# Halving the last units of a graph-convolution kernel, and weighing three of its last pairs on VectorE

## The chip, the cores and the metric

The kernel runs on one core of one Trainium2 chip. The metric is device time in microseconds. The profile's times (us) are counted from the start of the profiled execution's span; the lines (L415 and so on) are those of the kernel before.

## The reference

```python
h = max(layernorm(x), 0)                       # x: 4096 x 64
support = h @ weight                           # 64 x 64
mask = (adj != 0)                              # adj: 4096 x 4096, 64 MB in float32
rank = cumsum(mask, axis=1); deg = rank[:, -1:]
k = min(deg, 100); pos = rank - (deg - k)
w = mask * where(pos > 0, 0.5 ** (k - pos), 0)
out = x + w @ support + bias
```

A neighbour of a row therefore has a weight that halves with every later neighbour in that row: the last one weighs 1, the one before it 1/2, and those beyond the hundredth from the end nothing. To know the weight of a column one must know how many neighbours follow it, so the columns are worked from the right.

## The kernel before

**Units.** The 4096 rows form 8 groups of 512. Each group is worked in two units of 2048 columns, the right half first (L81), which makes 16 units, 0 to 15. A unit is loaded as four tiles of 128 rows by 2048 columns (1 MB each), so there are 64 tiles, 0 to 63. Unit 14 is the right half of the last group and unit 15 the left half.

**One unit's stages, with the function, line and engine of each.**

1. *load* (L118, SyncE's DMA queue) brings a tile into one of the 8 buffers of `apool`. A buffer is free again once its tile has been converted.
2. *convert* (L339, VectorE) turns float32 into bytes. For the tile numbers in `signed` it is L337 on ScalarE instead.
3. *transpose* (L350, TensorE) and *settle* (L361, VectorE) turn the bytes by 90 degrees, so that columns lie on partitions, and bring them back from PSUM to SBUF. PSUM tiles of tag "t" for this and for the next stages come from two banks, used in turn.
4. *totals* (L367, TensorE) counts neighbours in blocks of columns. *split* (L377, ScalarE) and *divide* (L380, VectorE) fetch one byte plane each of the same PSUM bank; in the program one of them always waits for the other. For a left half *carry* (L386, GpSimd) puts in the count of the right half, taken from `behind` of the unit before. *suffix* (L394, TensorE) and *clamp* (L398, VectorE) make from this `behind`, the number of later neighbours.
5. *place* (L405 and L410, TensorE) writes for four pairs at a time, 0 to 3 and then 4 to 7, a PSUM tile `v` whose bytes are the exponents. There are five banks for `v`, so the next place waits until three of the four pairs before it have been weighed.
6. *weigh* (L415, ScalarE) reads two byte planes of one `v`, 128 x 1024 elements, and writes exp(-ln 2 (38 + byte)), the weight, as `wk`. The factor 2 to the -38 is made good in the supports (L284). There are 8 pairs in a unit, 128 in all.
7. *aggregate* (L427, TensorE) multiplies `wk` with the supports `hr`, two matmuls to a pair, and adds up one group in the PSUM tile `acc`.
8. After a left half *drain* (L440), *turn_back* (L447) and *finish* (L454, L455) add the bias, turn the result back and add x. Only the last group does this in two halves of its rows: one drain on VectorE (L438), one on ScalarE (L440), and two stores (L457).

**What sets the order.** Each engine executes its instructions in the order in which they were written into the program. A list scheduler at the end of the function (L490 to L607) makes that order at build time: each task has an engine, a due time (its position in the stream of tiles, with the corrections in `shift` and `own`), costs in ns, and the tasks and buffers that it needs. It takes one task after the other and calls the functions in that order. None of this runs on the chip, so an instruction whose inputs are late holds up all that stand behind it on its engine.

Of the kernel before, what the change touches and what calls it, by code (L numbers as in the profile page):

```python
# [8 lines left out]
F32 = mybir.dt.float32  # L9
# [22 lines left out]
def kernel(  # L32
# [48 lines left out]
    UNITS = [(g, c * P * E, n) for g in range(G) for c, n in ((4, 4), (0, 4))]  # L81
# [4 lines left out]
    NP = 2 * CB  # L86
    NA = 8
# [21 lines left out]
    xt = apool.tile([P, N // H], F32, tag="a_sb", name="xt")  # L109
# [20 lines left out]
    junk = setup.tile([P, W], BF16, name="junk")  # L130
# [112 lines left out]
    def warm(n):  # L243

        for i in range(n):
            nc.tensor.matmul(none, junk[:, :P], junk, start=True, stop=True)  # L246
# [28 lines left out]
    def spread(n):  # L275
        if n == 0:
            pxs["var"] = ps_v.tile([P, W], F32, tag="v", name="pd")
        for b in range(4 * n, 4 * n + 4):
            nc.tensor.matmul(pxs["var"][:, H * b:H * (b + 1)], sq[:, b, :], ones, start=True, stop=True)  # L279
# [46 lines left out]
    masks, words, wts, accs, tots, pts, sums8, behind, vs, signed = {}, {}, {}, {}, {}, {}, {}, {}, {}, (2, 3, 5, 6, 12)  # L326
# [86 lines left out]
    def weigh(u, k):  # L413
        wts[u, k] = wpool.tile([P, 2, W], F32R, name="wk")
        nc.scalar.activation(wts[u, k], vs.pop((u, k)).bitcast(U8).rearrange("p (i f) -> p f i", f=4)[:, :2, :], AF.Exp, scale=-LN2, bias=floor)  # L415
# [5 lines left out]
    def aggregate(u, k):  # L421
# [3 lines left out]
        wk = wts.pop((u, k))  # L425
        for s in range(2):
            nc.tensor.matmul(accs[g], hr[:, block(u, k) + 4 * s, :, :].rearrange("p s d -> p (s d)"), wk[:, s, :],  # L427
                             start=(k == s == 0 and c0 + cb * E * P == N), stop=(c0 == 0 and (k, s) == (2 * cb - 1, 1)))
# [30 lines left out]
    def store(r):  # L459
# [8 lines left out]
    shift = {"aggregate": 56.5, "carry": -33, "center": -22.5, "clamp": -3, "constants": 17.5, "convert": 38.5, "drain": -32.5,  # L468
             "finish": -27, "first": -5.5, "order_of": -3, "place": 1, "power": -38.5, "relu": 13, "root": 21, "scale": 32.5,
             "second": 66, "settle": -19.5, "split": -26, "spread": -11.5, "square": 8.5, "suffix": 15.5, "support": 28.5,  # L470
             "totals": -2.5, "transpose": 1, "turn": 15, "turn_back": 55, "turned": 13.5, "weigh": 17.5}
    own = {
           "aggregate": {(0, 0): 6, (0, 1): 10, (0, 2): -1, (0, 4): -11, (0, 5): 21, (0, 6): -8, (0, 7): -1, (1, 0): -1, (1, 1): -1, (1, 3): 7, (1, 4): -8, (1, 5): -1},
           "carry": {(1,): -20}, "center": {(0,): 26, (1,): 62, (2,): 2, (3,): 1}, "clamp": {(0,): -2, (1,): 8, (2,): -1},
           "constants": {(0,): 5, (1,): -2},
           "convert": {(10,): -1, (11,): -16, (12,): -10, (13,): 12, (14,): -15, (15,): 12, (2,): 20, (3,): -8, (4,): -31, (7,): -6, (8,): -7, (9,): 2},
           "count": {(2,): 1, (4,): -10}, "counted": {(2,): -18, (4,): -19},
           "first": {(0, 0): -2, (0, 1): 19, (1, 0): -2, (1, 1): -9}, "order_of": {(2,): 4},
           "place": {(1, 0): 2, (1, 1): -8, (2, 0): 16}, "relu": {(0,): 24, (1,): 1, (3,): 2}, "root": {(): -17},
           "scale": {(1,): 12, (2,): 1, (3,): -5}, "second": {(0, 0): -2, (0, 1): -12, (1, 0): -5},  # L480
           "settle": {(0,): 5, (1,): -8, (10,): 5, (11,): 15, (12,): 4, (13,): 1, (14,): 21, (2,): -5, (3,): -8, (4,): 8, (5,): -4, (6,): -1, (7,): 24, (8,): 5, (9,): -2},
           "split": {(1,): 6, (2,): 2}, "spread": {(0,): -5, (1,): 1, (2,): 4, (3,): 1}, "square": {(0,): 2, (1,): 10, (2,): 4},
           "suffix": {(0,): -8, (1,): 20}, "support": {(0,): 5, (2,): -3, (3,): 8}, "totals": {(0,): 14, (1,): -8},
           "transpose": {(0, 2, 4): 4, (1, 0, 2): -3, (1, 2, 4): -6, (10, 0, 2): -7, (10, 2, 4): -6, (11, 0, 2): 16, (11, 2, 4): 5, (12, 0, 2): 8, (12, 2, 4): -5, (13, 0, 2): 8, (13, 2, 4): 4, (14, 0, 2): -1, (14, 2, 4): -8, (2, 0, 2): -11, (3, 0, 2): -2, (3, 2, 4): -4, (4, 0, 2): 26, (4, 2, 4): 19, (5, 0, 2): 6, (5, 2, 4): -3, (6, 0, 2): 4, (6, 2, 4): 14, (7, 0, 2): 14, (7, 2, 4): -1, (8, 0, 2): 4, (9, 2, 4): -6},
           "turn": {(0, 0): -2, (0, 12): 5, (0, 4): 5, (0, 8): 16, (1, 0): -10, (1, 12): -9, (1, 4): -8, (1, 8): 6},
           "turned": {(0, 12): 12, (0, 4): -4, (1, 0): 4, (1, 12): 16, (1, 8): 8},
           "weigh": {(0, 0): 11, (0, 1): -2, (0, 2): -4, (0, 3): -1, (0, 4): 8, (0, 6): 3, (0, 7): -1, (1, 0): -6, (1, 2): -18, (1, 3): 8, (1, 4): 4, (1, 6): -8}}
# [11 lines left out]
    for n in range(NT):  # L499
        slot = ("center", 3) if n == NA - 1 else ("convert", n - NA) if n >= NA else None  # L500
        task(load, (n,), SP, n, 0, 0, [slot])
# [143 lines left out]
```

## Time and profile before

| | |
|---|---|
| median of 8 runs | 193.39 us (192.66 to 195.26) |
| the profiled execution's own time | 192.9 us |
| its span, first to last instruction | 191.2 us |
| what lies around the span | 1.7 us |
| busy in the span | TensorE 171.0, ScalarE 167.4, VectorE 153.7, GpSimd 12.9 us |
| bytes moved | 69.47 MB, some 420 GB/s until 165 us |
| last convert (L339) | 168.10 to 169.48 us |
| first stores of the last group are issued | 187.99 us |

Busy time says how long an engine had an instruction in work, not that it set the time. A wait is named by what the engine waited for last. The chain that ended last is followed back from the last instruction to what released it.

### The profile page before, as it was taken

Reading aid. Unit: us, or ns where it says so; the run is one execution under the profiler, and the core shown is the slowest. Engines: PE = TensorE matmul, PEld = TensorE weight load, DVE = VectorE, ACT = ScalarE, POOL = GpSimd, SP = SyncE. Lnnn points to the kernel's source line nnn. Section 1 sums busy time; section 2 is a strip of 40 time slices with the busy share of each in tenths; the row PEclk is TensorE's granted clock in tenths of the full one; section 3 lists DMA queues with packets and bytes.
Section 4 is the critical chain, followed back from the end, with each engine's and each line's share of the span. In section 5 each row is a group of like instructions: output and inputs, shape, how many; then the busy total and the mean of one; then the engine's idle time right before and its main releaser. Section 6 shows DMA issues by size and latency. Waiting matters only on the chain.

```text
span 191.2 us, 3737 instructions
## 1 busy us (share of the span) xinstructions
PE 171.0 (89%) x1473; PEld 101.3 (53%) x1475; DVE 153.7 (80%) x213; ACT 167.4 (88%) x178; POOL 12.9 (7%) x54
## 2 busy tenths in 40 slices
PE   7799995979999998799999997999999889998961
PEld 2475982445546564556455555465555444664630
DVE  4852469999999988998899979999998999954012
ACT  2379988889899999999969999898699999989970
POOL 7000240200010002000010010000100100001000
PEclk9999999999999999999999999999999999999995
DMA  6999999999999999999999999999999999800100
GB/s 219 423 420 423 417 422 422 418 415 423 418 418 420 423 418 420 420 417 423 422 417 422 420 420 422 418 420 420 420 417 417 423 417 420 337 16 4 78 0 27
DMA packets 10337, 69.47 MB, mean 363 GB/s; under 512 B 1360, under 2 KB 1616, under 8 KB 2128
## 3 DMA queue, kind: packets, MB, share of 16 engines
q1 hardware_dynamic: 10016, 69.15, 87.4%
q8 instruction: 11, 0.18, 0.4%
q10 hardware_dynamic: 304, 0.10, 0.2%
q14 instruction: 6, 0.05, 0.1%
HBM read 68.19 MB, written 1.05 MB: 362 GB/s over the span
## 4 chain that ended last, share of the span: by engine, by line
PE 38%; DVE 33%; ACT 16%; issue 8%; POOL 3%; ACTq 0%; POOLq 0%; DVEq 0%
DVE m L339 16%; PE acc L427 14%; ACT wk L415 11%; PE pt L350 8%; DVE mt L361 6%; PE v L410 4%; PE v L405 4%; ACT sums L377 2%; DVE behind L398 2%; PE pc L263 2%; DVE sums L380 2%; PE pd L279 2%; PE tot L367 2%; PE po L447 1%; ACT xt L258 1%
## 5 line engine op out<-in xcount | busy, mean ns | idle before, releaser
L415 ACT ACTIVATE wk<-v,floor 128x1024 fp32r<-128x1024 uint8 x128 | 132.8, 1123 | 6.8 <-PE v L410 6.5
L339 DVE TENSOR_SCALAR m<-a_sb 128x2048 uint8<-128x2048 f32 x59 | 81.6, 1388 | 5.4 <-DMA a_sb<-in_adj_dram 5.4
L427 PE MATMUL acc<-wk,hr 128*128 128x512 f32 x256 | 77.9, 423 | 1.6 <-ACT wk L415 0.5
L427 PEld LDWEIGHTS acc<-wk,hr 128*128 128x128 f32 x256 | 43.8, 189 | 15.2 <-issue 5.0
L350 PE MATMUL pt<-ident,m 128*128 128x128 f32 x256 | 41.5, 282 | 6.5 <-DVE mt L361 2.9
L361 DVE COPY mt<-pt 128x512 uint32<-128x512 uint32 x59 | 40.2, 682 | 5.7 <-PE pt L350 5.7
L350 PEld LDWEIGHTS pt<-ident,m 128*128 128x128 f32 x256 | 27.8, 141 | 26.6 <-issue 9.8
L405 PE MATMUL v<-behind,where 32*128 32x512 f16 x128 | 15.6, 382 | 1.4 <-DVE behind L398 1.4
L386 POOL COPY sums<-behind 1x512 f16<-1x512 f16 x8 | 5.6, 706 | 141.1 <-ACT sums L377 141.1
L380 DVE CAST sums<-tot 128x512 f16<-128x512 uint8 x16 | 10.9, 683 | 4.9 <-ACT sums L377 4.2
L410 PE MATMUL v<-mt,tri 32*32 32x512 f16 x512 | 14.3, 394 | 0.0
L337 ACT ACTIVATE m<-a_sb 128x2048 int8<-128x2048 f32 x5 | 12.6, 2519 | 0.3 <-DMA a_sb<-in_adj_dram 0.3
L398 DVE TENSOR_SCALAR behind<-ps,excess 128x512 f16<-128x512 f32 x16 | 11.9, 742 | 1.2 <-PE ps L394 1.2
L377 ACT ACTIVATE sums<-tot 128x512 f16<-128x512 uint8 x16 | 9.6, 597 | 2.7 <-DVE sums L380 2.3
L394 PE MATMUL ps<-sums,later 128*128 128x512 f16 x32 | 9.7, 381 | 1.5 <-POOL sums L386 1.4
L367 PE MATMUL tot<-mt,band 128*32 128x512 f16 x128 | 10.2, 392 | 0.4
L410 PEld LDWEIGHTS <-tri 32*32 32x32 f16 x512 | 4.4, 88 | 10.3 <-issue 10.3
L246 PE MATMUL none<-junk 128*128 128x512 bf16 x24 | 8.1, 480 | 1.3 <-DVE junk L131 1.2
L405 PEld LDWEIGHTS <-where 32*128 32x128 f16 x128 | 3.6, 91 | 9.5 <-issue 9.3
L258 ACT ACTIVATE xt<-px 64x512 f32<-64x512 f32 x8 | 4.2, 586 | 4.6 <-PE px L254 4.6
L438 DVE TENSOR_SCALAR acc_part<-acc,bias_sb 128x256 f32<-128x256 f32 x1 | 0.5, 484 | 9.5 <-PE acc L427 9.5
L447 PE MATMUL po<-ident,acc_sb 128*128 128x128 f32 x30 | 4.9, 285 | 2.6 <-ACT acc_sb L440 2.5
(82 smaller groups left out, 82.0 us busy)
## 6 DMA issues: line engine op xcount, KB each, us to landing
a_sb<-in_adj_dram SPq DMA_DIRECT2D x64, 1024.0 KB, 16.2
xr<-in_x_dram SPq DMA_DIRECT2D x2, 512.0 KB, 6.2
out_dram<-xr SPq DMA_DIRECT2D x1, 512.0 KB, 18.6
out_dram<-xr SPq DMA_DIRECT2D x1, 384.0 KB, 2.3
out_dram<-xr ACTq DMA_DIRECT2D x1, 64.0 KB, 1.6
out_dram<-xr SPq DMA_DIRECT2D x1, 64.0 KB, 1.6
w<-in_L_gnn_weight_dram ACTq DMA_DIRECT2D x2, 16.0 KB, 5.7
bias_sb<-in_L_gnn_bias_dram SPq DMA_DIRECT2D x1, 0.2 KB, 17.4
```

The costliest lines, as they stand in the source:

```text
L337: nc.scalar.activation(m_v.bitcast(I8), a_v, AF.Sign)
L339: nc.vector.tensor_scalar(m_v, a_v, 0.0, 64.0, op0=ALU.not_equal, op1=ALU.add)
L350: nc.tensor.transpose(pts[n][:, c, :], m32[:, c * P:(c + 1) * P], ident)
L361: nc.vector.tensor_copy(mw, pt)
L367: nc.tensor.matmul(tot[SUB * c:SUB * (c + 1), :], band[:, SUB - 12 - 4 * a:2 * SUB - 12 - 4 * a], masks[u][:, c, :, a], start=(a == 0), st ...
L377: nc.scalar.activation(*bytes_of(u, 0), AF.Copy)
L380: nc.vector.tensor_copy(*bytes_of(u, 1))
L398: nc.vector.tensor_scalar(behind[u], pts.pop((u, "s")), excess[UNITS[u][2]], float(MAX_NEIGH), op0=ALU.subtract, op1=ALU.min)
L405: nc.tensor.matmul(v, where[q, a, :], behind[u][q, :], start=True, stop=False, skip_group_check=True)
L410: nc.tensor.matmul(vs[u, 4 * a + j][SUB * c:SUB * (c + 1), :], tri[q, q], m, start=False, stop=True, skip_group_check=True)
L415: nc.scalar.activation(wts[u, k], vs.pop((u, k)).bitcast(U8).rearrange("p (i f) -> p f i", f=4)[:, :2, :], AF.Exp, scale=-LN2, bias=floor)
L427: nc.tensor.matmul(accs[g], hr[:, block(u, k) + 4 * s, :, :].rearrange("p s d -> p (s d)"), wk[:, s, :], start=(k == s == 0 and c0 + cb * ...
```

## The change

- **Units.** The left half of the last group is cut into two units of 1024 columns: columns 1024 to 2047 (unit 15) and 0 to 1023 (unit 16). Each has four pairs and four tiles of 128 x 1024 (512 KB), so there are now 17 units and 68 tiles, 60 to 67 being half tiles. The second unit width brings a second set of small constants (`thr2`, `later2`, `excess2`) in the setup.
- **Weighing on VectorE.** Three pairs, number 4 of unit 14 and number 0 of units 15 and 16 (`QUICK`), are not weighed on ScalarE. VectorE makes their weights in three steps: *encode* computes max(-2^23 byte, -100 2^23) as int32 from PSUM, *cut* adds 100 2^23, and the result read as float32 is 2 to the (-27 - byte), or 0 from byte 100 on; *take* copies it to `wk`. As this is 2^11 more than ScalarE's weight, *lower* on GpSimd makes copies of their supports times 2^-11, six small instructions. The aggregate of these pairs is called *gather* in the scheduler, and stands at a place of its own.
- **Halves of the rows.** Pairs 2 and 3 of unit 16 (`PARTED`) are weighed and aggregated in two halves of 256 rows: half 0 of both, then half 1 of both.
- **Drains.** The last group's ScalarE drain now comes first, and VectorE's waits for it; before it was the other way round.
- **Elsewhere.** `signed` is (6, 15) and was (2, 3, 5, 6, 12), so ScalarE converts two tiles and not five. `xt`, the turned x, lies in a buffer of the mask pool instead of `apool`, so tile 7's load waits for no buffer. The matmuls on `junk` that keep TensorE busy are half as wide and end at the first *spread*; the variance's PSUM tile is taken from another pool. All numbers of `shift` and `own` are new, so the order of nearly all instructions moves by a little.

```diff
-    UNITS = [(g, c * P * E, n) for g in range(G) for c, n in ((4, 4), (0, 4))]
+    UNITS = [(g, c * P * E, n) for g in range(G) for c, n in (((4, 4), (2, 2), (0, 2)) if g == G - 1 else ((4, 4), (0, 4)))]
...
+    QUICK = (U - 3, 4), (U - 2, 0), (U - 1, 0)
+    PARTED = 2, 3
...
-    xt = apool.tile([P, N // H], F32, tag="a_sb", name="xt")
+    xt = mpool.tile([P, CB, W, 2], F16, name="mt").rearrange("p c i e -> p (c i e)").bitcast(F32)
...
-            pxs["var"] = ps_v.tile([P, W], F32, tag="v", name="pd")
+            pxs["var"] = ps_a.tile([P, W], F32, tag="acc", name="pd")
...
-    def weigh(u, k):
+    def weigh(u, k, part=None):
+        r = slice(0, W) if part is None else slice(part * W // 2, (part + 1) * W // 2)
+        if not part:
+            wts[u, k] = wpool.tile([P, 2, W], F32R, name="wk")
+        v = vs[u, k] if part == 0 else vs.pop((u, k))
+        nc.scalar.activation(wts[u, k][:, :, r], v.bitcast(U8).rearrange("p (i f) -> p f i", f=4)[:, :2, r], AF.Exp, scale=-LN2, bias=floor)
+
+    def encode(u, k):
+
+        both = apool.tile([P, N // H], F32, tag="a_sb", name="code")
+        codes[u, k] = both.rearrange("p (n f i) -> p n f i", n=2, f=2)
+        nc.vector.tensor_scalar(codes[u, k][:, 0].bitcast(I32), vs.pop((u, k)).bitcast(U8).rearrange("p (i f) -> p f i", f=4)[:, :2, :],
+                                -2.0 ** 23, -100 * 2.0 ** 23, op0=ALU.mult, op1=ALU.max)
+
+    def cut(u, k):
+
+        nc.vector.tensor_scalar(codes[u, k][:, 1].bitcast(I32), codes[u, k][:, 0].bitcast(I32), 100 * 2.0 ** 23, None, op0=ALU.add)
+
+    def take(u, k):
         wts[u, k] = wpool.tile([P, 2, W], F32R, name="wk")
-        nc.scalar.activation(wts[u, k], vs.pop((u, k)).bitcast(U8).rearrange("p (i f) -> p f i", f=4)[:, :2, :], AF.Exp, scale=-LN2, bias=floor)
+        nc.vector.tensor_copy(wts[u, k], codes.pop((u, k))[:, 1])
+
+    def lower(u, k):
+
+        if not low:
+            both = apool.tile([P, N // H], F32R, tag="a_sb", name="low").rearrange("p (n s e d) -> p n s e d", s=2, e=2, d=D)
+            low.update((uk, both[:, i]) for i, uk in enumerate(QUICK))
+        for s in range(2):
+            nc.gpsimd.tensor_scalar(low[u, k][:, s, :, :], hr[:, block(u, k) + 4 * s, :, :].bitcast(F32), 2.0 ** -11, None, op0=ALU.mult)
...
+            if (u, k) in QUICK:
+                weighs = "take"
+                task(encode, (u, k), DVE, due - 8, 1150, 1270, [("place", u, k // 4), ("convert", NT - 2)])
+                task(cut, (u, k), DVE, due - 8, 650, 770, [("encode", u, k)])
+                task(take, (u, k), DVE, due - 8, 650, 770, [("cut", u, k)], ("w", ("gather", u, k)))
+                task(lower, (u, k), POOL, due - 8, 1200, 1300, [("second", piece_of // 2, piece_of % 2), ("convert", NT - 3)])
...
+        for part in range(2 if u == U - 1 else 0):
+            for k in PARTED:
+                due = at + k + part
+                task(weigh, (u, k, part), ACT, due + 2.5, 520, 650, [("place", u, k // 4)], None if part else ("w", ("aggregate", u, k, 1)))
+                task(aggregate, (u, k, part), PE, due + 14, 260, 500, [("weigh", u, k, part)])
```

The order that results at the end is, on each engine (a pair is written unit.number, and "a/b" is half a or b of its rows):

- ScalarE: ..., 13.4, split 14, 13.5, 13.6, 13.7, 14.0, split 15, 14.1, drain of group 6, 14.2, 14.3, 14.5, split 16, 14.6, 14.7, 15.1, 15.2, 15.3, 16.1, 16.2 a, 16.3 a, 16.2 b, 16.3 b, drain.
- VectorE: convert 58, settle 57, convert 59, settle 58, convert 60, convert 61, settle 59, convert 62, settle 60, divide 14, settle 61, convert 63, clamp 14, settle 62, convert 64, settle 63, convert 65, settle 64, divide 15, settle 65, convert 66, convert 67, settle 66, finish of group 6, settle 67, encode 14.4, divide 16, clamp 15, cut and take 14.4, encode 15.0, clamp 16, cut and take 15.0, encode, cut and take 16.0, drain.
- TensorE, leaving out the transposes before tile 64: ..., place 14 (first), transpose 64, totals 15, aggregate 13.6, transpose 65, aggregate 13.7, transpose 66, turn_back of group 6, transpose 67, place 14 (second), totals 16, suffix 15, aggregate 14.0 to 14.3, place 15, suffix 16, gather 14.4, aggregate 14.5 to 14.7, place 16, aggregate 15.1, gather 15.0, aggregate 15.2, 15.3, 16.1, 16.2 a, 16.3 a, 16.2 b, gather 16.0, 16.3 b, turn_back.

## The prediction

> **What bounds the kernel now.** I read the page's slices first, then busy time by stretches, the costliest groups, and the timeline of the last 30 us.
>
> ```profile
> DVE  4852469999999988998899979999998999954012
> ACT  2379988889899999999969999898699999989970
> ...
> GB/s 219 423 420 423 417 422 422 418 415 423 418 418 420 423 418 420 420 417 423 422 417 422 420 420 422 418 420 420 420 417 417 423 417 420 337 16 4 78 0 27
> ```
>
> Until slice 34 (163 to 167 us) the load stream sets the pace: 420 GB/s without a gap, so a 1 MB tile each 2.50 us and a unit each 9.98. Tile 55's convert waits for its data at 147.92; tiles 59 and 63 thus land at 157.9 and 167.9. A gap there would cost, but the queue has 8 buffers (16.2 us from issue to landing, 2.5 to move), so what the change moves in the head is covered. Then come 23 us of tail. Busy time there, in stretches (PE, PEld, DVE, ACT, POOL):
>
> ```profile
> 165.00:171.00 6.00, 5.96 (x65) 3.81 (x64) 4.99 (x6) 5.55 (x6) 0.00 (x0) 1.00 0.26 104
> 171.00:185.00 14.00, 12.48 (x90) 7.39 (x89) 2.30 (x4) 13.45 (x14) 0.60 (x1) 1.00 0.07 28
> ```
>
> From 171 on ScalarE works 13.45 of 14 us and VectorE only 2.30. ScalarE's timeline (start, us, instruction, idle before it):
>
> ```profile
> 162.88 0.60 ACT L377 ACTIVATE sums<-tot 128x512 f16<-128x512 uint8 x1 [0.51 <-DVE sums L380]
> 163.37 7.18 ACT L415 ACTIVATE wk<-v,floor 128x1024 fp32r<-128x1024 uint8 x7
> 171.11 1.11 ACT L415 ACTIVATE wk<-v,floor 128x1024 fp32r<-128x1024 uint8 x1 [0.55 <-PE v L410]
> ...
> 174.16 10.44 ACT L415 ACTIVATE wk<-v,floor 128x1024 fp32r<-128x1024 uint8 x10
> ```
>
> The seven are 13.5 to 13.7 and 14.0 to 14.3; 14.0 starts at 163.37 + 3 x 1.036 = 166.48. The last weigh ends at 184.6, its aggregate at 185.38; from there drains, turn back, finish and store take 5.8 us to the span's end, 191.2. So the tail is ScalarE's 16 weighs from 166.48 on.
>
> ```profile
> L415 ACT ACTIVATE wk<-v,floor 128x1024 fp32r<-128x1024 uint8 x128 | 132.8, 1123 | 6.8 <-PE v L410 6.5
> L339 DVE TENSOR_SCALAR m<-a_sb 128x2048 uint8<-128x2048 f32 x59 | 81.6, 1388 | 5.4 <-DMA a_sb<-in_adj_dram 5.4
> L398 DVE TENSOR_SCALAR behind<-ps,excess 128x512 f16<-128x512 f32 x16 | 11.9, 742 | 1.2 <-PE ps L394 1.2
> ```
>
> These are the rows I price by: mean ns after the busy time.
>
> **What the skill says.** "VectorE: DVE Perf Modes", The perf-mode tier table: a copy or tensor_scalar in float32 from SBUF to SBUF does two elements a cycle (2048 in 1227 ns), with a PSUM operand in 4-byte types one. The trace agrees: L339 needs 0.68 ns an element in all, L398 and L361 from PSUM cost 742 and 682 ns for 512. "ScalarE: Activation LUTs", What ACT_TABLE_LOAD costs: an activation with a pointer as bias takes 280 + 0.833 N ns, and two in a row overlap by 93. The trace: 1123 for 1024, 704 for 512 (L440), and weighs start 1.036 apart. "GPSIMD Engine Reference", Specifications: GpSimd shares its SBUF interface with VectorE's two-port modes; carry took 603 to 1068 ns here, so some of that shows.
>
> **Prices.** Weigh 1.036. Half weigh 0.704 - 0.093 = 0.61. One element a cycle is 1.03 ns (L454's 256 in 421, L361's 512 in 682). Encode: L398's 0.742 and 512 elements more, 1.27. Cut and take, 1024 in SBUF: at most L339 less 512 cycles, 1.39 - 0.53 = 0.86; by the skill's row 1227 - 533 = 0.69 (an estimate). I take 0.75; if they ran at one element a cycle, 1.27. They depend on one another, so nothing overlaps. Half convert 1.30 - 0.53 = 0.77 from start to start, half settle 0.33. Lower: L296's 128x32 took 0.29, so six of 128x128 cost at most some 2.4 us of GpSimd, which idles 19.8 us before its last carry: nothing.
>
> **ScalarE's sum.** Three weighs go, -3.11. Split 16 comes, +0.49 (L377's spacing). Halves: 4 x 0.61 - 2 x 1.036 = +0.37. Net -2.25 us. The three converts off ScalarE (2.52 each) were at 17 to 47 us, long before; VectorE takes them at 1.30 in a head where it waited 4.6 us for a tile. Both lie under the load stream; they would cost only if a backlog of the head lasted to tile 56, and each unit leaves ScalarE and VectorE some 0.7 us to catch up.
>
> **Where part of it is lost.** I follow the new order of the engines, with the times of before as start.
>
> (a) Unit 14 starts later. VectorE now has converts 60 and 61 ahead of settle 59, and convert 62 and settle 60 ahead of divide 14. Convert 59 starts at landing, 157.9; settle 58 159.2; converts 60, 61 159.8 to 161.3; settle 59 161.3; convert 62 161.9; settle 60 162.65; divide 14 163.0 to 163.7 (before: 162.17). Split 14 waits for it: 163.7, not 162.88; 13.5 starts at 164.2 and 14.0 at 167.3: +0.8. Suffix, clamp 14 (165.0) and place 14, which needs 13.6 weighed (166.3), are ready at 167.0, just in time.
>
> (b) Split 15 waits for divide 15, behind settle 64, behind convert 65: 168.9, where 14.0 was done at 168.35: 0.55 idle. This takes the place of the 0.55 before 171.11.
>
> (c) 14.1 169.4, drain 170.4, 14.2 171.0, 14.3 172.05. Place 14 (second) needs 14.2: 172.15, done by 172.8; 14.5 at 173.1, no wait. Encode 14.4 at 173.1 (settle 67 is out of the way at 173.2), to 174.4. Split 16 174.15, then divide 16 174.8 and clamp 15 175.4 to 176.15: clamp 15, which all of unit 15 waits for, stands behind encode 14.4 and divide 16. Place 15 176.15, 15.1 at 176.8 (14.7 done 176.7; idle 0.1), 15.3 done 179.9.
>
> (d) VectorE from 176.1: cut, take 14.4 to 177.6; encode 15.0 to 178.7; clamp 16 to 179.4. TensorE has gather 14.4 and three aggregates ahead of place 16: 179.55 to 180.25. 16.1 at 180.15 (idle 0.2), halves from 181.2 to 183.75. VectorE: cut, take 15.0 to 180.8, encode, cut, take 16.0 to 183.6. Both engines end together; gather 16.0 183.65, last half aggregate 184.1 to 184.5 (184.2 if the dependent steps overlap by 0.1 each, as unrelated ones do).
>
> So the last aggregate ends 0.9 to 1.2 us earlier than 185.38; I take 1.05. The end after it is the same: two drains one after the other, only swapped, 256 rows each at 0.47 and 0.48. Span 190.15; that execution 192.9 - 1.05 = 191.85. The median stands 0.49 above the profiled execution: **193.39 - 1.05 = 192.3**.
>
> What hides what: the landing of tiles 60 to 67 (159.1 to 167.9) is ahead of their converts by 0.7 to 2.5 us, so half-sized loads cost nothing unless they are slower by more than that; the extra constants lie in the head's idle time. Carry 16 (0.6 to 1.1 us from 176.2) is hidden by encode 15.0 until 178.7, with cut and take beside it.
>
> **Rivals.**
>
> - *ScalarE's sum in full.* If 14.0 starts at 166.5 as before, say because ScalarE comes to unit 13 with less backlog, and VectorE's small steps are quicker than I took them: -2.25, 191.1. For it: VectorE did little in the tail before, and ScalarE is the bound. Against: split 14 already waited 0.51 us for VectorE, with one convert ahead of it and not three.
> - *VectorE becomes the bound (slower).* From clamp 15 to the last gather VectorE's steps stand in one chain: six cuts and takes, two encodes, clamp 16. Each 0.1 us on a cut or take is 0.6 us at the end; from 0.90 on (0.15 more than I took) the gain is gone, and at 1.27 gather 16.0 starts at 186.8, the last aggregate ends at 187.6, +2.2: 195.6. For it: no row shows int32 to int32 or a float32 copy to float32r in SBUF. Against: L339 changes type too and is fast, and L315 writes float32r at the plain price of a tensor_tensor (690 for 512).
> - *Nothing moves.* Cut and take at 0.86 and carry 16 delayed, or 4 KB rows that load more slowly and push (a): some 0.5 to 1 us, 193.0 to 193.4.
>
> **How the numbers follow.** My case (191.6 to 192.9) 0.40; full sum or near it (190.5 to 191.5) 0.27; nothing moves, up to 195 0.18; VectorE bound or a stall that I don't see, above 195, 0.15. About 1% (1.93 us) is what a measurement of this kernel can tell from no change. Below 191.46: 0.27. Above 195.32: 0.15. Between: 0.58. Range 190.7 to 194.7.
>
> **What would show it.** Right: split 14 and 15 wait for divide (L382); weighs of 14.0 start at about 167.3; encode near 1.27, cut and take near 0.75; the last take and the last half weigh end within 0.3 us of each other near 183.7. Wrong: cut or take above 0.9; ScalarE idle over 1 us after 168; the loads' end beyond 168.3; or 14.0 at 166.5 or earlier, which makes the first rival true.

## The result and the profile after

The changed kernel takes 198.04 us (median of 11 runs, 196.3 to 198.84), the kernel before, beside it, 193.44 (32 runs): ratio 1.021, 95% interval 1.017 to 1.024. It is slower by 4.6 us, where 1.1 us less were forecast, and lies outside the range.

The profiled executions took 198.82 us, with a span of 197.1, and before 192.9, with 191.2: 5.9 us apart, 1.3 more than the medians, so what the two profiles show between them is somewhat too large. First the slices of after, the lines that answer to those shown of before, and TensorE's granted clock:

```profile
DVE  3968188999989999999898899889988999998963
ACT  2463337999899999998898979897889789999970
...
PEclk9998569999999999999999999999999999999998
...
GB/s 222 425 421 421 419 422 417 422 416 424 417 419 419 424 419 421 422 419 419 422 416 424 424 421 417 422 419 419 419 421 422 407 314 219 211 7 80 0 3 27
```

Three things differ. The clock is at half speed around slices 4 and 5 (20 to 30 us), where it was full before. ScalarE does little in slices 3 to 5, and has more 7s and 8s after them than before had. The loads slow down from slice 32 on (314, 219, 211). The load queue waits for VectorE's converts to free a buffer, 7.3 us the longest time (2.9 before), so I take this for a consequence of the lateness, not its cause.

The tail, by stretches (PE, PEld, DVE, ACT, POOL): VectorE, nearly idle there before, now works 12.68 of the 14 us, in part because converts that are late fall into this stretch.

```profile
165.00:171.00 6.00, 6.00 (x68) 3.60 (x52) 5.92 (x10) 5.60 (x7) 2.99 (x5) 1.00 0.80 225
171.00:185.00 14.00, 12.19 (x108) 6.26 (x108) 12.68 (x22) 13.04 (x15) 3.45 (x4) 1.00 0.12 45
```

ScalarE's timeline from unit 14's split on, as it was shown of before:

```profile
170.75 0.60 ACT L379 ACTIVATE sums<-tot 128x512 f16<-128x512 uint8 x1 [0.18 <-DVE sums L382]
171.24 4.17 ACT L420 ACTIVATE wk<-v,floor 128x1024 fp32r<-128x1024 uint8 x4
175.91 0.59 ACT L379 ACTIVATE sums<-tot 64x512 f16<-64x512 uint8 x1 [0.49 <-DVE sums L382]
...
181.54 2.10 ACT L420 ACTIVATE wk<-v,floor 128x1024 fp32r<-128x1024 uint8 x2
184.11 2.12 ACT L420 ACTIVATE wk<-v,floor 128x1024 fp32r<-128x1024 uint8 x2 [0.47 <-PE v L412]
```

The row of four at 171.24 holds 13.5 to 13.7 and then 14.0, so 14.0 starts at 171.24 + 3 x 1.02 = 174.3 us; before, it was 166.4. From there to the span's end it is 22.8 us, and it was 24.8. **The tail gained 2.0 us, and unit 14 starts 7.9 us later.** The prices of the new steps are in the groups of VectorE (busy, mean ns):

```profile
L426 DVE TENSOR_SCALAR code<-v 128x1024 int32<-128x1024 uint8 x3 | 3.6, 1216 | 0.0
L435 DVE CAST wk<-code 128x1024 fp32r<-128x1024 f32 x3 | 2.4, 791 | 0.1
L431 DVE TENSOR_SCALAR code<-code 128x1024 int32<-128x1024 int32 x3 | 2.0, 680 | 0.0
```

So I look ahead of the tail. I call a unit's *lag* the time from the landing of its last tile to its first weigh (us). For all runs alike I let tile n land at 147.9 + 2.497 (n - 55), which is the load stream of before. A lag holds the way through the stages as well as the backlog, so what counts is how it changes.

| lag of unit | 0 | 2 | 3 | 6 | 9 | 12 | 14 |
|---|---|---|---|---|---|---|---|
| before | 12.7 | 14.3 | 13.4 | 10.8 | 10.1 | 9.6 | 8.5 |
| after | 14.0 | 17.7 | 16.7 | 15.8 | 16.9 | 17.3 | 16.4 |

3.3 of the 7.9 us are there at unit 3. The other 4.6 arise afterwards: before made up 4.9 us from unit 3 to 14, after makes up 0.3.

*In the head*, ScalarE's waits up to 34 us are, after and then before (total, times, longest):

```profile
ACT xs L272 <- PE pc L265: 6.0, 4, 2.7
ACT sums L379 <- PE tot L369: 5.5, 1, 5.5
```
```profile
ACT xt L258 <- PE px L254: 4.6, 2, 3.6
ACT sums L377 <- DVE sums L380: 0.8, 1, 0.8
```

ScalarE waits for TensorE, which from 16 to 29 us is busy without a gap at a granted clock of 0.61 (in before it is busy 12.41 of these 13 us, at 1.00).

*In the steady state* ScalarE idles more than before. Its waits from 60 to 150 us, after and then before:

```profile
ACT wk L420 <- PE v L412: 5.9, 8, 1.2
ACT sums L379 <- DVE sums L382: 2.7, 5, 0.6
```
```profile
ACT wk L415 <- PE v L410: 4.3, 5, 1.6
ACT sums L377 <- DVE sums L380: 1.0, 2, 0.5
```

In after it idles at the same places in every two units. Its timeline over two of them:

```profile
114.22 1.12 ACT L420 ACTIVATE wk<-v,floor 128x1024 fp32r<-128x1024 uint8 x1 [1.21 <-PE v L412]
115.23 0.68 ACT L473 ACTIVATE acc_sb<-acc,bias_sb 128x512 f32<-128x512 f32 x1
115.80 2.13 ACT L420 ACTIVATE wk<-v,floor 128x1024 fp32r<-128x1024 uint8 x2
118.56 0.60 ACT L379 ACTIVATE sums<-tot 128x512 f16<-128x512 uint8 x1 [0.64 <-DVE sums L382]
119.05 5.13 ACT L420 ACTIVATE wk<-v,floor 128x1024 fp32r<-128x1024 uint8 x5
124.81 5.19 ACT L420 ACTIVATE wk<-v,floor 128x1024 fp32r<-128x1024 uint8 x5 [0.62 <-PE v L412]
129.89 0.59 ACT L379 ACTIVATE sums<-tot 128x512 f16<-128x512 uint8 x1
130.37 3.13 ACT L420 ACTIVATE wk<-v,floor 128x1024 fp32r<-128x1024 uint8 x3
134.71 1.12 ACT L420 ACTIVATE wk<-v,floor 128x1024 fp32r<-128x1024 uint8 x1 [1.22 <-PE v L412]
```

It comes round after 134.71 - 114.22 = 20.49 us, 2.48 of them idle (0.64, 0.62, 1.22); the loads bring two units in 19.97. The 1.21 is a place that waits for a clamp, which stood behind a convert; the 0.62 a place that stood behind the aggregate of the pair just weighed; the 0.64 a split that waits for divide.

### The profile page after: what moved, and what is told of

The parts are those of the page before. It is cut to its first block, busy times and chain, and to the rows that moved or that the text cites. A ratio compares the mean times of both kernels' runs of the same rounds, so it can differ in the third digit from the quotient of the medians.

```text
span 197.1 us, 3798 instructions
## 1 busy us (share of the span) xinstructions
PE 177.3 (90%) x1494; PEld 106.0 (54%) x1494; DVE 169.6 (86%) x242; ACT 158.5 (80%) x175; POOL 23.2 (12%) x64
## 4 chain that ended last, share of the span: by engine, by line
PE 31%; DVE 26%; ACT 18%; issue 15%; POOL 4%; DMA 3%; SPq 0%; ACTq 0%; DVEq 0%; POOLq 0%
ACT wk L420 12%; DVE m L341 11%; PE acc L457 10%; DVE mt L363 5%; PE pt L352 4%; DVE sums L382 4%; PE v L412 3%; DMA xr<-in_x_dram 3%; ACT sums L379 3%; PE pd L281 3%; PE pc L265 3%; PE v L407 2%; DVE behind L400 2%; ACT mt L260 2%; PE ps L396 2%
## 5 line engine op out<-in xcount | busy, mean ns | idle before, releaser
L420 ACT ACTIVATE wk<-v,floor 128x1024 fp32r<-128x1024 uint8 (+1 forms) x127 | 130.6, 1107 | 10.2 <-PE v L412 10.2
L341 DVE TENSOR_SCALAR m<-a_sb 128x2048 uint8<-128x2048 f32 (+1 forms) x66 | 87.0, 1324 | 0.8 <-DMA a_sb<-in_adj_dram 0.8
L457 PE MATMUL acc<-wk,hr 128*128 128x512 f32 (+1 forms) x254 | 80.5, 426 | 3.8 <-ACT wk L420 3.8
L363 DVE COPY mt<-pt 128x512 uint32<-128x512 uint32 (+1 forms) x66 | 42.6, 650 | 6.2 <-PE pt L352 5.8
L352 PEld LDWEIGHTS pt<-ident,m 128*128 128x128 f32 x256 | 29.8, 145 | 18.9 <-issue 5.0
L388 POOL COPY sums<-behind 1x512 f16<-1x512 f16 x9 | 9.8, 1094 | 134.1 <-ACT sums L379 128.5
L379 ACT ACTIVATE sums<-tot 128x512 f16<-128x512 uint8 (+1 forms) x17 | 10.1, 593 | 10.4 <-PE tot L369 5.5
L382 DVE CAST sums<-tot 128x512 f16<-128x512 uint8 (+1 forms) x17 | 11.6, 685 | 5.2 <-ACT sums L379 4.6
L407 PE MATMUL v<-behind,where 32*128 32x512 f16 x128 | 14.4, 383 | 1.2 <-DVE behind L400 1.2
L412 PE MATMUL v<-mt,tri 32*32 32x512 f16 x512 | 14.3, 395 | 0.0
L396 PE MATMUL ps<-sums,later 128*128 128x512 f16 (+1 forms) x34 | 10.1, 379 | 2.0 <-POOL sums L388 1.6
L407 PEld LDWEIGHTS <-where 32*128 32x128 f16 x128 | 3.7, 91 | 11.8 <-issue 11.6
L248 PE MATMUL none<-junk 128*128 128x256 bf16 x38 | 6.3, 334 | 1.1 <-DVE junk L133 1.1
L248 PEld LDWEIGHTS <-junk 128*128 128x128 bf16 x38 | 4.5, 120 | 3.4 <-issue 1.1
```

The costliest lines, as they stand in the source:

```text
L341: nc.vector.tensor_scalar(m_v, a_v, 0.0, 64.0, op0=ALU.not_equal, op1=ALU.add)
L352: nc.tensor.transpose(pts[n][:, c, :], m32[:, c * P:(c + 1) * P], ident)
L363: nc.vector.tensor_copy(mw, pt)
L379: nc.scalar.activation(*bytes_of(u, 0), AF.Copy)
L382: nc.vector.tensor_copy(*bytes_of(u, 1))
L396: nc.tensor.matmul(px, later[cb][:r, f, :], sums[:r, f, :], start=(f == 0), stop=(f == 1))
```

## The experiments

All results in one table: median and ratio to before (95% interval), then, from the profiled execution, the lag of units 3 and 14, the start of 14.0, and the time from 14.0 to the span's end (us).

| run | us | ratio | unit 3 | unit 14 | 14.0 at | to the end |
|---|---|---|---|---|---|---|
| before | 193.4 | | 13.4 | 8.5 | 166.4 | 24.8 |
| after | 198.0 | 1.017 to 1.024 | 16.7 | 16.4 | 174.3 | 22.8 |
| tail_alone | 200.2 | 1.030 to 1.044 | 19.1 | 14.3 | 172.2 | 25.7 |
| no_tail | 200.1 | 1.029 to 1.040 | 16.0 | 15.4 | 173.3 | 25.2 |
| late_sums | 209.4 | 1.072 to 1.087 | 20.3 | 26.6 | 184.5 | 23.3 |
| warm_head | 195.8 | 1.012 to 1.016 | 15.8 | 13.9 | 171.8 | 22.8 |
| b_wait250 | 196.1 | 1.004 to 1.019 | 16.9 | 11.8 | 169.7 | 24.7 |
| head_undone | 196.9 | 1.010 to 1.021 | 18.9 | 15.2 | 173.1 | 22.3 |
| head_undone_400 | 199.4 | 1.019 to 1.037 | 19.7 | 18.7 | 176.5 | 22.5 |
| late_sums_drains | 206.0 | 1.057 to 1.069 | 17.1 | 22.0 | 179.9 | 24.4 |
| place_first | 196.8 | 1.010 to 1.022 | 15.8 | 14.1 | 172.0 | 22.8 |
| clamp_first | 200.5 | 1.024 to 1.040 | 14.2 | 16.3 | 174.2 | 22.8 |
| both_first | 198.6 | 1.020 to 1.031 | 15.9 | 16.1 | 174.0 | 22.8 |
| both_warm | 195.6 | 1.006 to 1.013 | 15.2 | 13.1 | 171.0 | 22.8 |
| splice | 200.4 | 1.023 to 1.040 | 14.6 | 16.1 | 174.0 | 22.8 |
| splice_const | 198.7 | 1.015 to 1.031 | 14.6 | 16.1 | 174.0 | 22.8 |
| splice_head | 204.8 | 1.047 to 1.065 | 18.5 | 21.1 | 179.0 | 22.8 |
| b_cold | 194.8 | 1.001 to 1.007 | 15.7 | 10.7 | 168.6 | 24.5 |
| tail_reordered | 192.6 | 0.993 to 0.997 | 15.0 | 9.6 | 167.5 | 23.3 |
| before_reordered | 193.8 | 0.998 to 1.004 | 15.7 | 10.0 | 167.9 | 23.9 |

**The tail alone, and all but the tail.** tail_alone takes from the changed kernel the head's edits (the diff below), the look-ahead of 250 ns and the new numbers of `shift` and `own`, so that before's numbers order the new tail. no_tail puts the old units back and empties `QUICK` and `PARTED`. By the traces, no_tail's ScalarE does the same in the same order as after's until the tail; tail_alone's order differs from before's from the head on, so it isn't before with nothing but a new tail.

```diff
-    ... signed = ..., (6, 15)
+    ... signed = ..., (2, 3, 5, 6, 12)
-    xt = mpool.tile([P, CB, W, 2], F16, name="mt")...
+    xt = apool.tile([P, N // H], F32, tag="a_sb", name="xt")
-    junk = setup.tile([P, 2 * P], BF16, name="junk")
+    junk = setup.tile([P, W], BF16, name="junk")
-            end = None if f is spread or end is None else at + tasks[f.__name__, *args][4]
+            end = None if f is aggregate or end is None else at + tasks[f.__name__, *args][4]
-            pxs["var"] = ps_a.tile([P, W], F32, tag="acc", name="pd")
+            pxs["var"] = ps_v.tile([P, W], F32, tag="v", name="pd")
```

> The kernel before with the edits of the tail alone: the two units of 1024 columns, the three pairs on VectorE, the halves of the rows, the swapped drains. The scheduler's numbers, the tiles that ScalarE converts, the place of xt and the warming matmuls are those of before. Theory A (the tail gains about 2 us, as the changed kernel's 22.8 us from the first weigh of unit 14 to the end against 24.8 before say; all of the loss arises ahead of unit 14): 191.2 to 191.9 us. Theory B (the tail's own steps cost the time: VectorE's chain, half-sized loads): 195 us or more.

> The changed kernel with the tail undone: 16 units, all pairs weighed whole on ScalarE; new scheduler numbers, two tiles converted on ScalarE, xt in the mask pool, half-wide warming matmuls. Theory A: about 2 us above the changed kernel, 199.5 to 200.5. Theory B: near the kernel before, 193 to 195.

tail_alone misses theory A by far. Its time lies in B's range, but most of the loss isn't B's: unit 14 starts 5.8 us later than before, and the tail is 0.9 longer (25.7 us; old numbers make a poor tail of the new tasks). Its first weigh is at 36.9 us (30.8 before), and the trace shows what stands ahead of it: ScalarE converts four tiles in a row from 20.44 us (9.51 us in all), and by the order of `signed` the first two are tiles 2 and 3, which unit 0 needs. Before's ScalarE starts these two at 13.19 and 17.43. no_tail hits A: the loss is there without the tail's edits, and with the new numbers they bring 200.1 - 198.0 = 2.1 us. In the profiles the tail is 2.4 us shorter (22.8 against 25.2), and unit 14 starts 1.0 later.

**The head.** warm_head puts back the wide matmuls on `junk` until the first aggregate, and the variance's old pool.

> The changed kernel with full-wide warming matmuls that go on until the first aggregate, as before, and the variance's PSUM tile in its old pool (the warming matmuls need the other one); the scheduler's order moves by a little with that. Theory A1: the head's TensorE clock stays at 1.0 (0.5 from 18 to 28 us in the changed kernel), the first weigh of unit 3 comes up to 2 us earlier, and the end by as much or less: 195.5 to 197. Theory A2 (all of the loss is the head): 191 to 193.

It is 2.2 us faster than after, as its first theory had it, but not by the head alone. Of the 2.5 us by which 14.0 is earlier, 0.9 are there at unit 3; the other 1.6 arise in units 3 to 13. The scheduler knows of the pool and orders the head and part of these units a little differently, so what the matmuls do by themselves isn't separated here.

**Look-ahead and numbers.** The look-ahead is the time by which the scheduler may put off an engine's next ready task for one that is due earlier; the first number is TensorE's.

```diff
-    wait = 400, 250, 250, 60, 0
+    wait = 250, 250, 250, 60, 0
```

> The kernel before with one number changed, the scheduler's look-ahead for TensorE (400 to 250 ns, as in the changed kernel). Its head is that of before, but the last pair aggregated ahead of a place is 3 weighs from that place's first one, and not 6 to 9. Theory C (an order that was planned this tightly can't make up a lag: in the changed kernel, in the one without the tail and in the one with wide warming the lag of the weighs stays at 14 to 17 us, in the two with the old numbers it shrinks by 0.5 us a unit): the lag of the weighs behind the loads stays near 12 to 14 us, where before it shrank to 8.5, and the time is 196 to 199 us. Theory D (the lag stays because of what the head does, not of the order): as before, 193 to 194.

> The changed kernel with its edits in the head undone (five tiles converted on ScalarE, xt in the load buffers, the variance's old pool, full-wide warming), its scheduler numbers and its tail kept. Last aggregated pair 3 to 6 weighs ahead of a place. Theory C: the head's lag is that of before or 1 us more, and shrinks little: 194 to 197. Theory D: 190.5 to 192.5, the head of before and the gain of the tail.

> The same as the kernel with the head undone, with the scheduler's look-ahead for TensorE at 400 ns as before: the last aggregated pair is 5 to 13 weighs ahead of a place. Theory C: the lag shrinks as before, by 0.4 to 0.5 us a unit, and the tail's gain comes to light: 190.5 to 192.5. Theory D: within 0.5 us of the one with 250 ns.

b_wait250 is 2.8 us slower than before. Its time is in theory C's range, but C's mechanism isn't there: the loss stands complete at unit 3 (3.5 us; here too ScalarE converts four tiles in a row, from 18.69 us), and behind it the units make up 5.1 us, where before makes up 4.9. head_undone, with the new numbers and 250, is in C's range as well, but makes up 5.7 us up to unit 12, and then loses 3.0 at unit 13. With 400 it is slower, not faster, and misses both theories. So neither the look-ahead nor the new numbers spoil the steady state by themselves; that the order comes out of all of them and of the head's tasks together is my reading.

**Aggregates later.** late_sums writes the aggregates of units 0 to 13 up to 3 us later, so that no place stands behind one that is just due. late_sums_drains moves them, and the drains, turn_backs and finishes of groups 0 to 6, by 2 us. In it a finish can be written behind the next use of its PSUM tile and then adds the wrong contents; its instructions are the same.

> The changed kernel, with the same order on all engines but one thing on TensorE: the aggregates of units 0 to 13 are written into the program up to 3 us later, so that a place no longer stands right behind the aggregate of a pair that ScalarE has just weighed (the last aggregated pair is 5 to 7 weighs ahead of the place's first one, not 2 to 3). Theory A1 (this closeness keeps ScalarE waiting 2.5 us in each two units and so keeps the lag of the head from shrinking, some 0.4 us a unit over 11 units): 193 to 195 us. Theory A2 (the lag comes from the head and stays whatever TensorE's order): 197 to 198.5.

> The changed kernel with the aggregates of units 0 to 13 written 2 us later on TensorE, and the drains, turn-backs and finishes of groups 0 to 6 as much later with them, since in the first such kernel ScalarE's drains waited 7.1 us for the late aggregates. The last aggregated pair is 4 to 5 weighs ahead of a place, not 2 to 3. Theory A1 (the closeness of aggregates and places is what keeps ScalarE waiting): the lag shrinks again, 193.5 to 196. Theory A3 (the tightness is in the whole order, VectorE's and ScalarE's too, and aggregates alone don't loosen it): 197 to 201.

Both miss both theories. ScalarE's waits from 60 to 150 us, late_sums first:

```profile
ACT acc_sb L473 <- PE acc L457: 7.1, 4, 2.3
```
```profile
ACT sums L379 <- DVE sums L382: 6.5, 6, 1.8
ACT wk L420 <- PE v L412: 6.4, 11, 1.3
```

The drain waits for the later aggregates; with the drains moved too, the wait comes back at split and place.

**Two neighbours exchanged.** Here I moved only what stands directly at the two waits of the steady state.

```diff
+    for u in range(3, 14):
+        for k in (0, 4):
+            at = when[place, (u, k // 4)]
+            for i, two in enumerate([(u, 2), (u, 3)] if k else [(u - 1, 6), (u - 1, 7)]):
+                if when.get((aggregate, two), at) < at:
+                    when[aggregate, two] = at[0], at[1] + 0.5 + 0.1 * i
...
+        if f is convert and u % 2 == 0:
+            when[convert, args] = at[0], at[1] + 0.5
```

> The changed kernel, in which only one thing is moved: for units 3 to 13, an aggregate of the third or fourth pair ahead of a place is written just behind that place (eight aggregates, at the first place of units 5 to 12); all else keeps its order. Theory S (the lag isn't made up in units 3 to 13 because two orders of neighbours each leave ScalarE idle: place behind the aggregate of the pair just weighed, 0.62 us every second unit, and clamp behind a convert, 1.21 us every second unit): four stalls of 0.62 go, the lag of unit 14 falls from 16.4 us to some 14, the time to 195 to 196.5. Theory T (these idle times only move; the rate is set by the sum of the work or by the loads): within 0.7 us of 198.0.

> The changed kernel, in which only one thing is moved: in units 4, 6, 8, 10 and 12, clamp is written just ahead of the convert that stood before it on VectorE. Theory S: five stalls of ScalarE of up to 1.21 us go, less what the place then waits for (0.3 us or so); the lag of unit 14 falls by 3 to 5 us, the time to 193.5 to 195.5. Theory T: within 0.7 us of 198.0.

> The changed kernel with both moves (the aggregates behind the places, the clamps ahead of the converts). Theory S: the two gains add up, as they are at different places: unit 14 at 168 to 170.5, the time 191.5 to 194.5, with a lag that shrinks by 0.4 us or more a unit as in the kernel before. Theory T: within 1 us of 198.0.

> The run warm_head (195.8 us: the changed kernel with the wide matmuls on junk up to the first aggregate and the variance's tile in its old pool) with both moves. Theory S: the head's 2.2 us and the steady state's gain add up until the lag is as small as before's: unit 14 at 166.5 to 168.5, then 22.8 us to the end of the span: 190.5 to 193, which would be level with or faster than the kernel before. Theory T: within 1 us of 195.8.

place_first removes the stalls of 0.62, as this row of ten weighs shows, where after has two rows of five:

```profile
117.37 10.26 ACT L420 ACTIVATE wk<-v,floor 128x1024 fp32r<-128x1024 uint8 x10
```

It is 1.3 us faster than after by the medians, just short of theory S, and its interval and after's overlap. Of the 2.3 us by which unit 14 is less late, 0.9 are there at unit 3, ahead of the edit; 1.4 arise behind it. clamp_first is 2.5 us slower than after, outside both theories' ranges. ScalarE's timeline of clamp_first:

```profile
113.15 1.12 ACT L420 ACTIVATE wk<-v,floor 128x1024 fp32r<-128x1024 uint8 x1 [0.80 <-PE v L412]
...
118.08 0.60 ACT L379 ACTIVATE sums<-tot 128x512 f16<-128x512 uint8 x1 [1.23 <-DVE sums L382]
```

The 1.21 became 0.80, and the 0.64 at split became 1.23: the convert that clamp passed is late for its own settle, totals and divide. From 60 to 150 us ScalarE's idle time grew from 8.6 to 10.7 us. So S falls for the clamps: the idle times moved, as T says, and grew. In both_first the clamps take back what the places gave (198.6), and both_warm is at 195.6: both hit T and miss S, and both_warm is only 0.2 us below warm_head.

**Orders written out.** In these kernels the scheduler's order is replaced by a list. splice takes before's order and head for units 0 to 12, after's behind it; splice_const has the second width's constants earlier; splice_head takes before's order for units 3 to 12 only. b_cold is before with the changed kernel's matmuls on `junk` alone.

```diff
+    written = """... 147510 settle 55; 148390 ..."""
+    order = []
+    for n, line in enumerate(written.split(";")):
+        at, f, *args = line.split()
+        order.append((int(at), n, called[f], tuple(map(int, args))))
```

> Before's order, written out as a list, for the head and units 0 to 12 (its signed tiles, its matmuls on junk, its place of the turned x), and behind it the changed kernel's order for units 13 to 16 with the half tiles, the three pairs on VectorE and the halves of the rows; the second width's constants are made at some 60 us, where no one waits for them. Theory P (the loss lies wholly in the order and the head ahead of unit 14, and the tail's edits gain what they were worked out to gain): 14.0 starts at 166.5 to 168, 22.8 us before the span's end; 191 to 193 us. Theory Q (the tail's edits themselves delay unit 14, for instance by the half tiles or by the waits of unit 13): 14.0 at 169 or later, 194 or more.

> The run splice with the second width's constants (a 128 by 128 set made on VectorE and GpSimd, a count on TensorE and its correction) made in the head, at the places where the changed kernel has them, some 8 to 13 us into the order. If they are what put tail_alone's first weigh 6 us later: first weigh at 33 to 37 us and 193 to 197. If they lie in idle time: within 0.5 us of splice.

> The changed kernel with its own head, units 0 to 2 and tail, but with before's order for units 3 to 12. If the order of units 3 to 12 is what fails to make up the lag: the lag of unit 3 is 15 to 17 us as in the changed kernel, that of unit 14 is 10 to 13, 14.0 at 168.5 to 171, 193 to 195.5 us. If the lag stays whatever the order (loads, sums of work): 197 to 198.5.

> The kernel before with one thing changed: its matmuls on junk are half as wide, twice as many, and end at the first spread, as in the changed kernel; its order is untouched. If these matmuls are the head's loss: TensorE's granted clock drops between 18 and 30 us, unit 3 starts 1.5 to 3 us later, of which units 3 to 13 make up a part or all, 193.5 to 195.5. If not: within 0.5 us of before.

splice lies in Q's range and misses P by its total, but not by its units: with before's order they make up the lag again, 14.6 at unit 3 to 11.6 at unit 10, as before does (13.4 to 9.3); at units 13 and 14 it rises, to 16.1. At the seam my list has an aggregate of unit 12 ahead of suffix 13 on TensorE, and it waits for a drain that stands behind split 13:

```profile
159.00 0.74 PE L457 MATMUL acc<-wk,hr 128*128 128x512 f32 x2 [2.50 <-ACT acc_sb L473]
```

That is a fault of the splice and no proof against P, nor for it. splice_const's first weigh is at 32.0 us, splice's at 31.9: the constants in the head cost nothing there. At unit 4 splice_const is even 1.1 us less late (13.2, 14.3), and its median is 1.7 us lower, which its theories don't explain. splice_head misses both theories: from unit 3 to 12 it makes up only 0.6 us (18.5 to 17.9), and then has the same bad seam, so before's order is no remedy behind this head. b_cold costs 0.4%, as forecast, and in its profile the clock falls to 0.6 in slices 4 and 5 and unit 3 is 2.3 us later; behind that it makes up 5.0 us, as before does, so this rate doesn't hang on the head's clock. Of its 20 runs 13 take over 194 us, of the 23 of before beside it 3; the others of both take 192.7 to 193.9. This looks as if the half-wide matmuls made the fall of the clock more frequent, and not as if they alone made it; one profile of each can't show that.

**An order that suits the edits.** Both last kernels keep before's head and order up to unit 9. From unit 10 on I searched the order anew, moving one task after the other in a replay of the engines with the traces' durations, once with the tail's edits and once without.

> Before's head and order up to unit 9, then the tail's edits (half tiles, three pairs on VectorE, halves of the rows), with the tasks from unit 10 on in an order searched anew with the durations of the traces. Theory P (the tail's edits cost nothing ahead of unit 14 if the order suits them): the lag of unit 14 is 8 to 10 us as in the kernel before, 14.0 starts at 165.5 to 168, 22.5 to 23 us to the span's end, 189.5 to 192 us. Theory Q (the tail's edits delay unit 14 in any order, by the half tiles or by what VectorE has more to do): 14.0 after 169, 193.5 or more.

> The control: the kernel before with no edit but the order of the tasks from unit 10 on, searched anew in the same way. What an order suited to it is worth without the tail's edits: 191.3 to 193 us. Theory P then has tail_reordered 1 to 3 us below this run; theory Q has tail_reordered at or above it.

192.6 us with the edits and 193.8 without are both above what P named (up to 192 and 193), but the mechanism is P's and not Q's: tail_reordered is the faster by 1.2 us, unit 14 has a lag of 9.6 and starts at 167.5, and from there it is 23.3 us to the end (up to 23 named). tail_reordered is 0.5% below before (ratio 0.995, 0.993 to 0.997), and 5.4 us below after. Its ScalarE, from unit 14's split on:

```profile
163.89 0.60 ACT L379 ACTIVATE sums<-tot 128x512 f16<-128x512 uint8 x1 [0.56 <-DVE sums L382]
164.39 6.20 ACT L420 ACTIVATE wk<-v,floor 128x1024 fp32r<-128x1024 uint8 x6
170.46 0.70 ACT L473 ACTIVATE acc_sb<-acc,bias_sb 128x512 f32<-128x512 f32 x1
...
176.76 3.13 ACT L420 ACTIVATE wk<-v,floor 128x1024 fp32r<-128x1024 uint8 x3 [0.26 <-PE v L412]
180.31 3.43 ACT L420 ACTIVATE wk<-v,floor 128x1024 fp32r<-128x1024 uint8 x5 [0.43 <-PE v L412]
```

14.0 is the fourth of the six, 164.39 + 3 x 1.03 = 167.5; the last half weigh ends at 183.7.

## Why the prediction was wrong

**The step that failed** is "Both lie under the load stream; they would cost only if a backlog of the head lasted to tile 56, and each unit leaves ScalarE and VectorE some 0.7 us to catch up", and with it "what the change moves in the head is covered". Three parts of it were wrong.

1. *The backlog does last to tile 56, in before too.* I read the pace from loads without a gap and from converts that wait for their data. But the weighs of before start 13.4 us behind the landing at unit 3 and still 8.5 at unit 14. The converts' waits, 5.4 us in the row that the prediction shows, were misread: by before's trace 4.8 of them lie in the first 30 us, and then VectorE waits for a tile once, 0.5 us, at tile 55. The loads never stop because 8 buffers take them in; ScalarE and what feeds it set the pace, at 9.5 us a unit. How much of the 8.5 is backlog isn't known, but it hasn't come to rest: b_cold is 2.3 us later than before at unit 3 and still 2.2 at unit 14.
2. *The head isn't free of change.* Unit 3 is 3.3 us later in the profile. In these profiles the granted clock has the largest share: clamp_first has the same head, in its execution at full clock, and is 2.5 us less late there (14.2, which leaves 0.8 to before). But before loses this at times too (its order and head ran at 0.6 in before_reordered, 15.7 at unit 3), so it is a difference of executions as well as of kernels, and one profile doesn't say how much of the medians' difference it makes.
3. *The catching up is no property of the engines' load, but of the order.* I counted on 0.7 us of each unit from busy times and took the new numbers as "the order of nearly all instructions moves by a little". From unit 4 to 13 both kernels do the same work, and before makes up 0.45 us a unit, after 0.03. That is 4.6 of the 7.9 us by unit 14, the largest term of the miss. That it is the order is shown as far as before's order makes up 5.0 us from a later start too (b_cold), so that neither the lateness nor the clock decides it; but from unit 3 to 12 behind after's head it makes up only 0.6 (splice_head).

**What held.** The tail, nearly as worked out: from 14.0 to the span's end 22.85 us were expected and 22.8 measured. That they agree so closely is in part luck. The last aggregate ends 17.5 us after 14.0 and not 17.0, since ScalarE waits 0.47 us for place 15 and 0.43 for place 16, where 0.1 and 0.2 were expected; and from its end to the span's end it is 5.3 us and not the 5.8 of before. With ScalarE's drain first, the first half is turned back while VectorE drains the other (192.34 and 192.32 us), where before's first turn back waited for both drains (186.53, the second drain from 186.00); so the swap, which I put at nothing, gained. Encode 1.27 expected, 1.22 measured; half converts 0.77 from start to start and 0.65 (173.03 to 173.68 us); cut and take 0.75, and 0.68 and 0.79 in the mean. For cut and for the second and third take (0.69 each) the estimate from the Trainium skill, "VectorE: DVE Perf Modes", The perf-mode tier table, two elements a cycle and so 0.69 us, was nearer than mine; the first take took 0.98. So VectorE didn't become the bound: that rival stood on cuts and takes of 0.90 on average, and the slower result has another mechanism. Step (b) held too (0.49 idle at split 15, 0.55 expected). Of the signs given for "wrong" the loads' end came true, which moved past 168.3 (slice 34, from 167.5 us on, still has 211 GB/s), and one take of three was above 0.9. ScalarE's idle times from 168 us to its last weigh are 1.6 us in all, none over 0.5. No sign looked at the steady state.

**What is shown and what is open.** Shown: the tail's edits are worth 2.1 us with after's numbers (no_tail against after) and 1.2 in orders searched for each (193.8 against 192.6; how good each search was isn't known); the loss lies ahead of unit 14. Shown for parts of it: the matmuls on `junk` and the variance's pool with the order that comes of them, 2.2 us (warm_head). Likely, but within the intervals: eight aggregates ahead of their places, 1.3 (place_first). The parts don't add up: with all of them both_warm has 195.6. Not settled: which of the new numbers, the look-ahead and the moved conversions makes the order of units 3 to 13 so that nothing is made up. The numbers with before's head did make it up until unit 12, before's numbers with 250 did too, and only together with the new head they don't. The first weigh at 36.9 us in tail_alone goes with ScalarE's late converts of tiles 2 and 3, as far as the trace shows; no run moved them, and for head_undone it stays open.

## What to carry to other kernels

Loads without a gap don't say that the loads set the pace: measure how far the last stage runs behind the landing, unit by unit, and whether that distance ever comes to rest; as long as it doesn't, a delay of the head can arrive at the end (here 2.3 us became 2.2). A change that gives a scheduler new numbers is a change to the whole kernel, and its rate of catching up is to be compared before its tail is priced. Where engines wait for one another in a fixed order, moving one instruction ahead of another can move the wait to whatever the other one feeds, so look at both.

## What was not expected of the hardware

- TensorE's granted clock fell to 0.5 to 0.6 in the head while TensorE was busy without a gap (13.00 of 13.00 us from 16 to 29 us in after). It fell in before_reordered too, which has the head that before's profile shows at 1.00, and it stayed at 1.00 there in clamp_first, which has the head of after. What brings it down isn't shown. A row of twelve 128x128 transposes took 2.99 us at the low clock (at 23.60), one of eight took 1.09 at full clock (at 104.10).
- Cut, int32 to int32, took 0.67 to 0.69 us for 1024 elements, and take, float32 to float32r, 0.69 (2 of 3). Encode, with as many elements from PSUM, took 1.22, which is 0.53 more; 512 times the prediction's 1.03 ns an element is 0.53 too. So cut and take fit two elements a cycle where encode fits one.
- The first take took 0.98 us and not 0.69. GpSimd's carry ran beside it, from 183.14 to 184.08, and took 0.94 us; before's last carry, at 172.77 us beside a divide that reads PSUM, took 0.60. This agrees with the Trainium skill, "GPSIMD Engine Reference", Specifications, where GpSimd shares its SBUF interface with VectorE's two-port modes. Which of the two loses is not always the same: in tail_reordered the first cut and take took 0.68 and 0.67, and two of *lower*'s instructions beside them 2.41 us, where its other two pairs took 1.03 and 1.01.

```profile
183.14 0.94 POOL L388 COPY sums<-behind 1x512 f16<-1x512 f16 x1 [5.59 <-DVE behind L400]
```
```profile
183.64 0.98 DVE L435 CAST wk<-code 128x1024 fp32r<-128x1024 f32 x1
```
